# First layers of q and k as seven block products, v centered in its weights, and a plan ranked by kinds of steps

## The chip, the cores and the metric

The kernel runs on one core of a Trainium2 chip. The metric is the device time of that core in microseconds, the median of several runs. The engines are called PE (TensorE, the matrix engine), DVE (VectorE), ACT (ScalarE), POOL (GpSimd) and SP (SyncE, which here only issues transfers). PEld is PE's loading of weights, which overlaps its matmuls. All data is float32.

## The reference

The input x has 4 sequences of 2048 tokens with 256 values each. Two layers follow each other, each added to its input and normalized.

```python
def _mlp(x, W1, b1, W2, b2):
    h = gelu(x @ W1 + b1)                     # exact gelu
    return h @ W2 + b2
q, k, v = _mlp(x, W1q, ...), _mlp(x, W1k, ...), _mlp(x, W1v, ...)
scores = (q @ k.T) / sqrt(256 * 512) * tril(ones)      # causal, without softmax
out = scores @ v
out = (out - mean(out)) * rsqrt(var(out) + 1e-5) * ln_w + ln_b
x = layernorm(x + out)

xn = layernorm(x) * ln_gamma + ln_beta         # soft mixture of 16 experts, 16 slots each
logits = unit(xn) * scale @ unit(mu)           # 256 logits a token
dispatch = softmax(logits over the 2048 tokens of a sequence)
combine  = softmax(logits over the 256 slots)
slot_in  = dispatch.T @ xn
slot_out = gelu(slot_in @ w1[e] + b1[e]) @ w2[e] + b2[e]
x = layernorm(x + combine @ slot_out)
```

The sequence is the unit over which tokens are dispatched: a slot sums over all tokens of one sequence.

## The kernel before

The 8192 tokens are worked in 16 groups of 512 (`W`), four to a sequence; a group is four chunks of 128 tokens (`G = 4`, `P = 128`). Everything is written once as steps, and a planner in the kernel's Python code (`Plan`) decides in which order the steps of each engine are emitted; on the chip each engine works through its own list strictly in that order and waits on semaphores.

**The planner.** `plan.step(engine, length, emit, reads, writes, ...)` records a step with an assumed duration. `plan.begin(base)` sets the rank from which the following steps count up by 0.01; a step that reads a PSUM bank gets 1.5 less. `run` repeatedly takes, for each engine, the ready step with the smallest key: its possible starting time plus `PATIENCE[engine]` times its rank, then the rank. `LATE` is the assumed delay until another engine sees a step's end, `TABLE` the price of switching ScalarE's function table. `plan.tag` gives a kind of buffer its places, and a step that needs a buffer waits until one is free. PSUM has eight banks: three `mm`, two `tp`, three `at`.

**A group, in `attend`.** `load_x` brings the group's rows (`row`) and, by eight block transfers, the same tokens in a form that DVE's 32x32 transpose (L795) turns into `xT`, 128 input values by 512 tokens in two halves. L810 multiplies `xT` by W1q, W1k and W1v: for each of them two output halves `m`, each a sum over two input halves `k`, with 512 tokens as the moving side:

```python
for k in range(KC):
    nc.tensor.matmul(ph.place, wa[f"W1{n}"][:, k, m * P : (m + 1) * P], xT[:, k, :],
                     start=(k == 0), stop=(k == KC - 1))
```

L820 reads the bank with bias and gelu on ACT into `hid`. The second layers of q and k are folded into one matrix (`fold`, `wqk_sb` in `both_sb`), so that L833 makes `kt` from hidden k, and q is hidden q itself. L843 adds on DVE. `turn_group` sends `kt` through a bounce in DRAM (SP) and DVE's transpose (L542) back as `kT`. L860 and L871 make `vt`. L885 gives the scores of a chunk with itself, masked by L896. Everything before the chunk comes from running states: L912 multiplies `kt` and `vt`, L928 adds to `state`; L945 and L954 sum the bias's part of a chunk, which goes through DRAM and back into `a` and `run` (L960 to L969), where POOL adds (L979). L995 and L999 make the output of a chunk, L1010 adds it to `a`, L561 and L562 (`means`) take its mean and variance on DVE, and L1022 centers it and multiplies by `lnw`.

**The rest of a group.** `norms`: POOL adds `ln_b` to the row (L1041), takes roots by a power (L550), DVE joins (L1064), the next norm follows (L561 again, or, for the last two groups, squares on ACT at L571), centering on ACT and DVE (L664, L669), then gamma and beta on POOL (L1127, L1139) and squares on ACT (L1155). `back`: the logits (L1201), DVE's scaling (L1211), the smallest (L1223), and ACT's exponentials for combine (L1234), which go through DRAM. After each fourth group `softmaxes` (L1312, L1324), `slots` (L1346 sums the slots' inputs, then the experts) and `finish` (L1572 combines, L1580 adds, the last norm, the store).

**What sets the order around the change.** PE's list mixes groups: while one group's first layers run, the earlier group's scores, states and logits are interleaved. SP's list holds all transfers in one order. At the start, `load_x(0)`, the weights (W1q and W1v, W2q from ACT's queue, W1k, W2k, W2v from SP's), `load_x(1)`, `fold` (L746, L754, L768, L778), `unit_mu` (L704, L712, L691, L730) and `load_experts` come, each with its rank.

Of the kernel before, what the change touches and what calls it, by code (L numbers as in the profile page):

```python
# [8 lines left out]
F32 = mybir.dt.float32  # L9
# [5 lines left out]
P = 128  # L15
G = 4
# [9 lines left out]
LAST = 2  # L26
PART = 2
# [29 lines left out]
class Plan:  # L57
# [4 lines left out]
    PATIENCE = {"PE": 0.0, "DVE": 0.0, "ACT": 0.0, "POOL": 0.0, "SP": 0.5, "IN": 0.0}  # L62

    def __init__(self):
        self.steps, self.places, self.order, self.free = [], {}, {}, set()
        self.base = self.count = 0.0

    def begin(self, base):

        self.base, self.count = base, 0.0  # L70

# [13 lines left out]
    def step(self, engine, length, emit, reads=(), writes=(), table=None, holds=(), port=False):  # L85
# [3 lines left out]
        s = Step(engine, length, emit, self.base + self.count, table)  # L89
        s.holds = list(holds)  # L90
# [4 lines left out]
        if any((a[0] if isinstance(a, tuple) else a).tag.startswith("ps_") for a in reads):  # L95
            s.rank -= 1.5
        for accesses, write in ((reads, False), (writes, True)):
# [24 lines left out]
    def run(self):  # L122
# [26 lines left out]
        while left:  # L149
# [38 lines left out]
            free[e] = end  # L188
# [39 lines left out]
def kernel(  # L228
# [43 lines left out]
    for tag, n, shape in (  # L272
        ("row", 8, [G, C + 1]),
        ("xT", 2, [KC, W]),
        ("hid", 5, [KC, W]),
# [10 lines left out]
        ("lg", 7, [G, ES]),  # L286
        ("mx", 1, [ES]),
        ("ct", 5, [EH, W]),
# [20 lines left out]
    bank_places("mm", 3)  # L309
    bank_places("tp", 2)  # L310
    at_banks = bank_places("at", 3)
# [4 lines left out]
    def load_x(t):  # L316
# [15 lines left out]
        plan.step("SP", {0: 2.5, 1: 6.0, 2: 4.0}.get(t, 0.5), emit, writes=[xt])  # L332
# [5 lines left out]
        xs = plan.buffer("xT", KC)  # L338
# [14 lines left out]
        plan.step("SP", 4.8, emit_blocks, writes=[xs])  # L353
# [14 lines left out]
    )  # L368
    mu_sb = const.tile([P, KC, ES], F32, name="mu_sb")
# [29 lines left out]
    def load_experts():  # L399
# [20 lines left out]
        for n, length, emit in (  # L420
            ("w1", 7.0, emit_w1), ("w2", 2.2, emit_w2), ("b2", 10.1, emit_b2)
        ):
            plan.tag(n, [w1_sb])
            arrivals[n] = plan.buffer(n)
            plan.step("SP", length, emit, [], [arrivals[n]])
# [3 lines left out]
    for n, after in (  # L429
# [5 lines left out]
        plan.step("IN", after, lambda: None, [], [arrivals[n]])  # L435
    plan.tag("wqk", [mu_sb])
    arrivals["wqk"] = plan.buffer("wqk")
# [49 lines left out]
    def flips(src, at=None, dst=None):  # L487

        for h in range(2):
            pt = plan.buffer("ps_tp")  # L490
# [8 lines left out]
            plan.step("PE", G * _FLIP, flip, [src], [pt], holds=[dst] if dst else ())  # L499
            yield h, pt  # L500

    def transpose_group(src, dst, engines, at=None):
        for h, pt in flips(src, at, dst):
# [3 lines left out]
            plan.step(engines[h], length, emit, [pt], [(dst, [h])])  # L507
# [12 lines left out]
    def turn_out(src, of=None):  # L520
# [7 lines left out]
        plan.step("SP", 0.65 * (2 if of else 1), emit, [src], [bounce])  # L528
        return bounce

    def turn_in(bounce, dst):
# [8 lines left out]
        plan.step("SP", 2.2, emit, [bounce], [dst])  # L540
        plan.step(
# [4 lines left out]
    def inv_root(v, n):  # L546
# [7 lines left out]
        plan.step("POOL", 1.04 if n == G else 0.75, emit, [v], [r])  # L554
        return r

    def means(src, st, mv, c, access):
# [6 lines left out]
        plan.step("DVE", 0.6, emit, [src], [(st, [c]), (mv, [c])])  # L564

    def squares_of(src, mv, c, access):
# [9 lines left out]
        plan.step("ACT", 0.6, emit, [src, (mv, [c])], [(mv, [G + c])])  # L576

    def root_of(mv, cs, factor, add):
# [12 lines left out]
        plan.step("POOL", 0.25, emit, [(mv, cs)], [negm])  # L591
# [12 lines left out]
        plan.step(  # L604
# [5 lines left out]
    def center_by(dst, r, nm, engines, c0=0):  # L610

        for i, engine in enumerate(engines):
# [14 lines left out]
            plan.step(  # L627
# [6 lines left out]
    def center(dst, mv, r):  # L634

        for c in range(G):
# [7 lines left out]
            plan.step("DVE", 0.42, emit, [mv, r], [(dst, [c])])  # L644

    def center_on(dst, mv, r, engines, c0=0):
# [4 lines left out]
        plan.step(  # L651
# [7 lines left out]
        for i, engine in enumerate(engines):  # L659
# [14 lines left out]
            plan.step(  # L674
# [4 lines left out]
    def spread(col):  # L679
# [7 lines left out]
        plan.step("DVE", 0.56, emit, [col], [dg])  # L687
# [8 lines left out]
        plan.step("PE", _pe(ES), emit, [dg], [row])  # L696
        return row

    def unit_mu():
# [6 lines left out]
        plan.step("POOL", 1.1, emit, [muw], [mu2], port=True)  # L706
# [10 lines left out]
        plan.step("PE", 0.9, emit, [mu2], [pss])  # L717
# [6 lines left out]
        plan.step("DVE", 0.17, emit, [pss], [ms])  # L724
# [9 lines left out]
        plan.step("DVE", 0.96, emit, [row], [muw])  # L734

    def fold():
# [3 lines left out]
        for i, n in enumerate(("W2q", "W2k")):  # L740
            pt = plan.buffer("ps_tp")
# [9 lines left out]
            plan.step("PE", 4 * _FLIP, emit, [arrivals[n]], [pt])  # L751
# [10 lines left out]
            plan.step("DVE", 0.7 + 0.1 * (not i), emit, [pt], [f])  # L762
        for m in range(KC + 1):
# [11 lines left out]
            plan.step("PE", 2 * _pe(C + 1), emit, [f], [pw])  # L775
# [6 lines left out]
            plan.step("DVE", _dve(C), emit, [pw], [arrivals["wqk"]])  # L782

    a_tiles, n_tiles, l_tiles, c_tiles, t_tiles = {}, {}, {}, {}, {}
    state, run = [None], [None]

    def attend(t):
# [3 lines left out]
        if t in xs_tiles:  # L791

            xT = xs_tiles.pop(t)
            plan.step(
# [3 lines left out]
        else:  # L798
            xT = plan.buffer("xT", KC)
            transpose_group(xt, xT, ("DVE", "ACT"))  # L800

        hid = {}
        for i, n in enumerate("qkv"):
            hid[n] = plan.buffer("hid", KC)
            for m in range(KC):
                ph = plan.buffer("ps_mm")

                def emit(n=n, m=m, ph=ph):
# [6 lines left out]
                plan.step(  # L815
                    "PE", KC * _pe(W), emit, [xT, arrivals[f"W1{n}"]], [ph], holds=[hid[n]]
                )

                def emit(i=i, n=n, m=m, ph=ph):
                    nc.scalar.activation(  # L820
                        hid[n][:, m, :], ph.place, AF.Gelu,
                        bias=cols_sb[:, 4 * i + m : 4 * i + m + 1],
                    )

                plan.step("ACT", _act(W, 1), emit, [ph], [(hid[n], [m])], table="gelu")
        qT = hid["q"]
        kt = plan.buffer("kt", G)
        for c in range(G):
            pk = plan.buffer("ps_mm")

            def emit(c=c, pk=pk):
                for k in range(KC):
                    nc.tensor.matmul(  # L833
                        pk[:, : C + 1], hid["k"][:, k, c * P : (c + 1) * P], wqk_sb[:, k, :],
# [3 lines left out]
            plan.step(  # L838
                "PE", 2 * _pe(C + 1), emit, [hid["k"], arrivals["wqk"]], [pk], holds=[kt]
            )  # L840
            plan.step(
# [12 lines left out]
        for c0 in range(0, G, 2):  # L854
            pv = plan.buffer("ps_mm")

            def emit(c0=c0, pv=pv):
                for j in range(2):
                    for k in range(KC):
                        nc.tensor.matmul(  # L860
                            pv[:, j * C : (j + 1) * C],
                            hid["v"][:, k, (c0 + j) * P : (c0 + j + 1) * P],
# [3 lines left out]
            plan.step(  # L866
# [810 lines left out]
```

## Time and profile before

| what | value |
|---|---|
| median of 3 runs | 657.66 us (657.54 to 657.99) |
| span of the profiled execution, its own time | 656.7 us |
| busy PE, PEld, DVE, ACT, POOL | 644.6, 482.2, 482.8, 265.7, 308.6 us |
| L810, each of W1q, W1k, W1v | 128 instructions, 60.0, 58.2, 59.8 us |
| L820 ACT, 128x512, 96 times | 685 ns each |
| L1155 ACT, 128x256, and reading its accumulator, 64 times | 414 and 188 ns |
| L485 ACT copy of 128x512 | 589 ns |
| L928 DVE addition of 128x512, 56 times | 677 ns |
| L561, L562 DVE statistics on `a`, 64 times | 423 and 182 ns |
| L979 POOL addition of 128x256 | 741 ns |
| transfers | 85.24 MB, mean 130 GB/s |

The span runs from the first instruction to the last; the profiled execution has no other time of its own than this span, and the median of the runs is 1.0 us above it. A float32 matmul appears as two instructions. The mean duration that a group of matmuls shows includes the overlap of one with the next, so the price of one is read from a run of them in the chain of work that ended last.

### The profile page before, as it was taken

To read this page: it belongs to the slowest core of one execution; us is meant where nothing else is said; L and a number is where in the kernel's file an instruction comes from. 1 tells how busy PE (TensorE), PEld (TensorE's weight loads), DVE (VectorE), ACT (ScalarE), POOL (GpSimd) and SP (SyncE) were. 2 spreads that over 40 slices of the span, in tenths; PEclk is the share of its full clock that TensorE was granted. 3 is DMA by queue.
4 is the path that set the end of the run, shared out by engine and by line. 5 is a ranking of instruction groups with operands and counts; after the bars stand their busy time and mean duration, and the time that the engine had idled before them with its cause. 6 is when DMAs were issued, how large, how long until landed. Compare 5 with 4: busy or idle time off the path is not lost.

```text
span 656.7 us, 9472 instructions
## 1 busy us (share of the span) xinstructions
PE 644.6 (98%) x2964; PEld 482.2 (73%) x2964; DVE 482.8 (74%) x1295; ACT 265.7 (40%) x610; POOL 308.6 (47%) x407
## 2 busy tenths in 40 slices
PE   8999999999999999999999999999999999999995
PEld 6667767676768876857776877777776877887874
DVE  1448696868782987788796498688979689875686
ACT  3121343325255227051627212624244634536575
POOL 4415825251529145643517503757252927547234
PEclk9999999999999999999999999999999999999998
DMA  8967567765864267966677352794969672310374
GB/s 247 207 147 205 112 149 118 145 113 123 140 145 78 54 107 224 195 124 126 128 146 137 72 117 52 225 204 96 152 136 156 109 153 50 78 35 1 78 148 160
DMA packets 326458, 85.24 MB, mean 130 GB/s; under 512 B 257292, under 2 KB 324168, under 8 KB 326408
## 3 DMA queue, kind: packets, MB, share of 16 engines
q1 hardware_dynamic: 325304, 83.58, 60.5%
q10 hardware_dynamic: 960, 0.80, 0.4%
q8 instruction: 23, 0.38, 0.3%
q0 software_dynamic: 144, 0.26, 0.1%
q14 instruction: 27, 0.22, 0.1%
HBM read 52.57 MB, written 32.04 MB: 129 GB/s over the span
## 4 chain that ended last, share of the span: by engine, by line
PE 92%; ACT 1%; DVE 1%; DMA 1%; issue 1%; SPq 1%; POOL 1%; POOLq 0%; DVEq 0%; ACTq 0%
PE mm L810 25%; PE mm L1201 8%; PE at L1346 8%; PE mm L833 8%; PE at L912 8%; PE mm L860 8%; PE at L995 7%; PE at L1572 6%; PE at L885 4%; PE at L999 4%; PE at L945 1%; ACT squares L571 1%; DMA row<-in_x_dram 1%; DMA xnT<-bounce 1%; POOL root L601 1%
## 5 line engine op out<-in xcount | busy, mean ns | idle before, releaser
L820 ACT ACTIVATE hid<-mm,cols_sb 128x512 f32<-128x512 f32 x96 | 65.0, 685 | 194.2 <-PE mm L810 194.0
L550 POOL TENSOR_TENSOR root<-ve,nhalf 128x4 f32<-128x4 f32 (+1 forms) x39 | 41.2, 1058 | 143.8 <-DVE ve L1054 55.5
L995 PE MATMUL at<-state,hid 128*128 128x256 f32 x240 | 61.6, 379 | 0.0
L810 PE MATMUL mm<-xT,W1v_sb 128*128 128x512 f32 x128 | 59.8, 593 | 0.7 <-DVE both_sb L778 0.7
L912 PE MATMUL at<-vt,kt 128*128 128x256 f32 x240 | 60.4, 384 | 0.0
L810 PE MATMUL mm<-xT,W1q_sb 128*128 128x512 f32 x128 | 60.0, 596 | 0.2 <-DVE xT L484 0.2
L833 PE MATMUL mm<-both_sb,hid 128*128 128x257 f32 x256 | 59.2, 380 | 0.0
L1346 PE MATMUL at<-row,lg 128*128 128x257 f32 x256 | 58.2, 381 | 0.4 <-ACT lg L1324 0.4
L860 PE MATMUL mm<-W2v_sb,hid 128*128 128x256 f32 x256 | 58.5, 379 | 0.0
L1201 PE MATMUL mm<-mu_sb,xnT 128*128 128x256 f32 x256 | 58.1, 380 | 0.3 <-DVE xnT L542 0.3
L810 PE MATMUL mm<-xT,W1k_sb 128*128 128x512 f32 x128 | 58.2, 592 | 0.0
L1572 PE MATMUL at<-so,ct 128*128 128x256 f32 x256 | 57.6, 380 | 0.1
L1234 ACT ACTIVATE xn<-lg,nrm 128x256 f32<-128x256 f32 x64 | 31.9, 499 | 61.8 <-DVE lg L1211 61.8
L1201 PEld LDWEIGHTS mm<-mu_sb,xnT 128*128 128x128 f32 x256 | 48.4, 190 | 10.3 <-issue 2.6
L1572 PEld LDWEIGHTS at<-so,ct 128*128 128x128 f32 x256 | 48.2, 190 | 9.7 <-DVE st L561 1.2
L833 PEld LDWEIGHTS mm<-both_sb,hid 128*128 128x128 f32 x256 | 48.3, 190 | 8.9 <-issue 1.6
L995 PEld LDWEIGHTS at<-state,hid 128*128 128x128 f32 x240 | 45.4, 190 | 12.1 <-issue 6.5
L1346 PEld LDWEIGHTS at<-row,lg 128*128 128x128 f32 x256 | 47.9, 190 | 8.4 <-ACT lg L1324 1.0
L912 PEld LDWEIGHTS at<-vt,kt 128*128 128x128 f32 x240 | 44.6, 190 | 12.2 <-issue 5.4
L860 PEld LDWEIGHTS mm<-W2v_sb,hid 128*128 128x128 f32 x256 | 48.3, 190 | 7.1 <-DVE vt L871 0.4
L1041 POOL TENSOR_TENSOR row<-row,rows_sb 128x512 f32<-128x512 f32 x32 | 38.1, 1210 | 16.8 <-DMA row<-in_x_dram 11.7
L1251 POOL TENSOR_TENSOR sum<-sum,ss 128x4 f32<-128x4 f32 x16 | 4.0, 252 | 85.9 <-DVE ss L1247 70.9
(150 smaller groups left out, 1220.5 us busy)
## 6 DMA issues: line engine op xcount, KB each, us to landing
bounce<-xn SPq DMA_DIRECT2D x30, 512.0 KB
row<-in_x_dram SPq DMA_DIRECT2D x16, 512.0 KB
ct<-bounce SPq DMA_DIRECT2D x64, 128.0 KB
xT<-in_x_dram SPq DMA_DIRECT2D x120, 64.0 KB
bounce<-kt SPq DMA_DIRECT2D x30, 256.0 KB
kT<-bounce SPq DMA_DIRECT2D x60, 128.0 KB
out_dram<-row SPq DMA_DIRECT2D x15, 512.0 KB
xnT<-bounce SPq DMA_DIRECT2D x56, 128.0 KB
```

Of the source, the lines that this page charges most:

```text
L550: nc.gpsimd.tensor_tensor(r[:, :n], v[:, :n], nhalf.to_broadcast([P, n]), ALU.pow)
L810: nc.tensor.matmul(ph.place, wa[f"W1{n}"][:, k, m * P : (m + 1) * P], xT[:, k, :], start=(k == 0), stop=(k == KC - 1),)
L820: nc.scalar.activation(hid[n][:, m, :], ph.place, AF.Gelu, bias=cols_sb[:, 4 * i + m : 4 * i + m + 1],)
L833: nc.tensor.matmul(pk[:, : C + 1], hid["k"][:, k, c * P : (c + 1) * P], wqk_sb[:, k, :], start=(k == 0), stop=(k == KC - 1),)
L860: nc.tensor.matmul(pv[:, j * C : (j + 1) * C], hid["v"][:, k, (c0 + j) * P : (c0 + j + 1) * P], wa["W2v"][:, k, :], start=(k == 0), stop=( ...
L912: nc.tensor.matmul(pds[:, m * C : (m + 1) * C], kt[:, c, m * P : (m + 1) * P], vt[:, c, :], start=True, stop=True,)
L995: nc.tensor.matmul(po[:, :C], qT[:, k, toks[c]], s[:, k, :], start=(k == 0), stop=False,)
L1041: nc.gpsimd.tensor_tensor(row[:, c : c + PART, :C], row[:, c : c + PART, :C], lnb_r[:, :PART], ALU.add,)
L1201: nc.tensor.matmul(pl[:, j * ES : (j + 1) * ES], xnT[:, k, (c0 + j) * P : (c0 + j + 1) * P], mu_sb[:, k, :], start=(k == 0), stop=(k == KC ...
L1234: nc.scalar.activation(by_halves(cb)[:, :, c, :], lg[:, c, :].rearrange("p (h e) -> p h e", h=EH), AF.Exp, bias=nrm[:, c : c + 1], scale=-1.0,
L1346: nc.tensor.matmul(psi[:, : C + 1], lg[:, c, h * P : (h + 1) * P], row[:, c, :], start=(i == 0), stop=(i == n - 1),)
L1572: nc.tensor.matmul(pc[:, :C], ct[:, h, c * P : (c + 1) * P], so_t[:, h, :], start=(h == 0), stop=(h == EH - 1),)
```

## The change

**Seven products.** From group 1 on (`FIRST = 1`) q's and k's first layers are made block by block. The weights of one projection are four blocks (two input halves `k` by two output halves `m`), the tokens of a group four blocks (two input halves by two halves `lo` and `hi` of 256 tokens). Instead of eight products of blocks, seven are made, of sums and differences of blocks, by the same trick for q and k at once, so that one bank holds 256 columns of q and 256 of k. `mix_weights` makes three mixed weight blocks per projection once (DVE), `mix_last` replaces one block of W1q and W1k after group 0. `mix_tokens` makes four differences of token blocks per group on POOL (one in place). `project_mixed` has the products: the bank `sums` gets products 1, 3, 5 and 6, one on top of the other, and between them ScalarE copies what is in it (`keep`), and at last reads it (`activate2`); the banks `one` (product 2) and `two` (4, 7) are added by DVE to the copies (`add`); the gelu then works on those in place. `hid` for q and k becomes `hqk`, with two places for both; v keeps L810's form and has two places.

**Centering v.** `center_v` subtracts from each row of W2v, and from b2v, its own mean, once. The mean of the attention's output over the 256 values is then zero: `means` on `a` and the subtraction of the mean go away. The variance is the sum of squares, made on ACT (`attend12`, with an accumulator) and divided by 256 in `norms3`; `attend13` only multiplies by `lnw`.

**The plan.** Each step has a name; `plan.begin` gives a phase too. A table `SHIFTS` adds a number to the rank of each kind of step. `PATIENCE` is now 0.035 for ACT (0 before) and 0 for SP (0.5 before). `OVERLAP` lets the next step of an engine begin a little before the end of the one before. The banks are four `mm`, one `tp`, three `at`; the second of two transposes uses an `at` bank. `lg` has 6 places for 7, `ct` 4 for 5. In the emitted order of SP all rows' loads and the experts' weights now come ahead of the first bounce of `kt`, and `b2`'s 16 loads ahead of the first return of the running sums.

```diff
+SHIFTS = {
+    "": {"load_experts1": -80.298},
+    "attend": {"activate1qk": 1.52, "activate2qk": 5.949, "activate3qk": -0.301,
...
+}
+FIRST = 1
+STR_V = False
+ACC = False
+TENG = 'POOL'
+MM, TP, AT = 4, 1, 3
...
-    PATIENCE = {"PE": 0.0, "DVE": 0.0, "ACT": 0.0, "POOL": 0.0, "SP": 0.5, "IN": 0.0}
+    OVERLAP = {"PE": 0.0, "DVE": 0.075, "ACT": 0.09, "POOL": 0.06, "SP": 0.0, "IN": 0.0}
+
+    PATIENCE = {"PE": 0.0, "DVE": 0.0, "ACT": 0.035, "POOL": 0.0, "SP": 0.0, "IN": 0.0}
...
+        s.rank += SHIFT.get(s.kind, 0.0)
...
-            free[e] = end
+            free[e] = max(at, end - self.OVERLAP[e])
...
-        ("hid", 5, [KC, W]),
+        ("hqk", 2, [2, KC, W]),
+        ("hid", 2, [KC, W]),
+        ("xs", 1, [3, W // 2]),
...
-        ("lg", 7, [G, ES]),
+        ("lg", 6, [G, ES]),
...
-        ("ct", 5, [EH, W]),
+        ("ct", 4, [EH, W]),
...
+    def mix_weights():
+        def emit(w, s):
+            for to, a, b, op in (
+                (s[:, 0, :], w[:, 0, P:], w[:, 1, P:], ALU.add),
+                (s[:, 1, :], s[:, 0, :], w[:, 0, :P], ALU.subtract),
+                (s[:, 2, :], w[:, 1, :P], s[:, 1, :], ALU.subtract),
+            ):
+                nc.vector.tensor_tensor(to, a, b, op)
...
+    def mix_tokens(xT):
...
+        less(1, y(0), x(0, hi), x(0, lo), [(xT, [0, 1])], [(xs, [0])])
+        less(2, y(1), x(1, hi), y(0), [(xT, [3]), (xs, [0])], [(xs, [1])])
+        less(3, x(0, hi), x(1, hi), x(0, hi), [(xT, [3])], [(xT, [1])])
+        less(4, y(2), x(1, lo), y(1), [(xT, [2]), (xs, [1])], [(xs, [2])])
...
+        def product(name, bank, weights, tokens, reads, new):
+            def emit():
+                for j, i in enumerate(ids):
+                    nc.tensor.matmul(
+                        bank[:, j * N : (j + 1) * N], weights(i), tokens(),
+                        start=(new and not j), stop=True, skip_group_check=True,
+                    )
...
+        product(f"1{part}", sums, own(0, 0), x(0, lo), given + [(xT, [0])], True)
+        product(f"2{part}", one, own(1, 0), x(1, lo), given + [(xT, [2])], True)
+        keep(f"1{part}", sums, 0, 0, lo)
+        add(f"1{part}", one, 0, 0, lo)
+        product(f"3{part}", sums, mixed(1), y(1), [wm, (xs, [1])], False)
+        keep(f"2{part}", sums, 0, 1, hi)
+        product(f"4{part}", two, mixed(0), y(0), [wm, (xs, [0])], True)
+        product(f"5{part}", sums, own(0, 1), x(0, hi), given + [(xT, [1])], False)
+        keep(f"3{part}", sums, 1, 1, hi)
+        add(f"2{part}", two, 1, 1, hi)
+        for i in ids:
+            activate(f"1{part}", i, 1, None, hi, [])
+        product(f"6{part}", sums, own(1, 1), y(2), given + [(xs, [2])], False)
+        product(f"7{part}", two, mixed(2), x(1, hi), [wm, (xT, [3])], False)
+        for j, i in enumerate(ids):
+            activate(f"2{part}", i, 1, lambda j=j: sums[:, j * N : (j + 1) * N], lo, [sums])
+        add(f"3{part}", two, 0, 1, hi)
+        for i in ids:
+            activate(f"3{part}", i, 0, None, slice(0, W), [])
...
+    def center_v():
+        w, b = wa["W2v"], rows_sb[:, 0, :]
...
-            means((a, [c]), st, mv, c, lambda c=c: a[:, c, :])
...
-                nc.vector.scalar_tensor_tensor(
-                    a[:, c, :], a[:, c, :], mv[:, c, 0:1], lnw_r[:, 0, :],
-                    ALU.subtract, ALU.mult,
-                )
...
+                nc.scalar.activation(
+                    squares.rearrange("p k d -> p (k d)"), a[:, c, :], AF.Square,
+                    accum_out=mv[:, c, 1:2],
+                )
+
+            plan.step("attend12", "ACT", 0.6, emit, [(a, [c])], [(mv, [c])])
...
+                nc.vector.tensor_tensor(a[:, c, :], a[:, c, :], lnw_r[:, 0, :], ALU.mult)
```

In the changed kernel's own lines, the products are L953, `keep` L969, `add` L976, the subtractions of `mix_tokens` L924, the gelu L1067, v's first layer L1080, `kt` L1111, the scores L1163, the squares of `a` L1308.

## The prediction

> **What bounds the kernel now.** I read the page first (busy shares, clock, chain), then the windows, then the chain in order of time for the price of one matmul, then the groups for the other durations.
>
> ```profile
> PE 644.6 (98%) x2964; PEld 482.2 (73%) x2964; DVE 482.8 (74%) x1295; ACT 265.7 (40%) x610; POOL 308.6 (47%) x407
> ...
> PEclk9999999999999999999999999999999999999998
> ...
> PE 92%; ACT 1%; DVE 1%; DMA 1%; issue 1%; SPq 1%; POOL 1%; POOLq 0%; DVEq 0%; ACTq 0%
> ```
>
> TensorE is busy for 98% of the span at the full clock, and 92% of the chain that ended last is TensorE. Nothing else is near: VectorE has 174 us idle, ScalarE 391 us.
>
> ```profile
> 400.00:500.00 100.00, 100.00 (x436) 73.60 (x435) 80.72 (x217) 39.60 (x88) 51.69 (x64) 1.00 0.73 152
> ...
> 640.00:657.00 17.00, 8.77 (x41) 7.38 (x39) 10.33 (x36) 9.88 (x31) 7.36 (x20) 0.86 0.44 155
> ```
>
> The columns are PE, weight loads, DVE, ACT, POOL. In the middle PE has no idle time; only the start and the last 8 us are not PE's. So a shorter PE sum shortens the kernel one for one, as long as nothing makes PE wait.
>
> ```profile
> 182.53 3.45 PE mm L1201 x16
> ...
> 188.47 3.43 PE mm L810 x8
> ```
>
> These are lines of the chain in order of time. Eight 512-column instructions take 3.43 us (0.429 each), sixteen 256-column ones 3.45 us (0.216 each): PE's time goes by columns, and half the width costs half. A float32 matmul is two instructions here: L810 has 64 W1q matmuls in the code and 128 in the page.
>
> **The sum of the PE work removed.** Before, q and k of one group are 2 x 4 matmuls of 512 columns: 16 instructions x 0.429 = 6.86 us. After, 2 x 7 of 256 columns: 28 x 0.216 = 6.05 us. That is 0.82 us a group; groups 1 to 15 have it: **-12.2 us**. The changed kernel's order on PE confirms the count: 72 matmuls of 512 columns for 192, 904 of 256 for 694, all other shapes equal. The 28 weight loads are 0.190 us each under matmuls of 0.216; the L1201 row is exactly such a stream (a new weight for every 256 columns), so no price is added there.
>
> **What goes to the other engines, per group.**
> ScalarE: three `keep` copies of 128x512 from PSUM, 0.589 each by the L485 copies: 1.77. Four 256-wide and two 512-wide activations stand for four 512-wide ones; a 256-wide one lies between the squares' 0.414 (L1155) and the exponentials' 0.499 (L1234), I take 0.457, the middle: 4 x 0.457 + 2 x 0.685 - 4 x 0.685 = +0.46. The squares of the attention output: 4 x (0.414 + 0.188 for reading the accumulator) = 2.41. Together 15 x 2.23 + 16 x 2.41 = 72 us: 266 becomes 338 us, 52%.
> VectorE: three adds of 128x512 at 0.677 (L928) are +2.03; four statistics pairs at 0.423 + 0.182 (L561, L562) are -2.42; four products with lnw at 0.473 (L1223) for 0.514 (L1022) are -0.16. With some 6 us of one-time mixing and centering the engine stays at about 480 us.
> GpSimd: four `less` subtractions, 0.741 each by L979: 15 x 2.96 = 44 us, so 353 us.
> None of the three comes near the 632 us that PE keeps. All this work is hidden by PE as long as the round trips below are; without that cover each group pays for its longest wait.
>
> ```profile
> 55.45 2.50 POOL L1041 TENSOR_TENSOR row<-row,rows_sb 128x512 f32<-128x512 f32 x2 [0.24 <-DMA row<-in_x_dram]
> 55.46 1.55 DVE L1064 SCALAR_TENSOR_TENSOR row<-a,root,row 128x256 f32<-128x256 f32 x1
> ```
>
> This timeline shows a DVE instruction of mean 0.517 us take 1.55 beside a POOL instruction that began 0.01 us before. If every new POOL instruction held DVE up for its whole 0.741 us, DVE would get 60 x 0.741 = 44 us more: 525 us, still 107 us under PE. I take a quarter of it, since most L1064 rows are not lengthened (the mean is 0.517), and price it at nothing for PE. The Trainium skill, SBUF — State Buffer, section SBUF: two separate sides, states that a DVE instruction with two SBUF inputs and a GpSimd instruction exclude each other on a shared port pair, the loser waiting for the whole instruction; it speaks against putting the subtractions on GpSimd, and by it the full 44 us would be the reading.
>
> **The new round trips.** The bank `sums` is used four times in a row: product 1, `keep1` on ScalarE, product 3, `keep2`, product 5, `keep3`, product 6, `activate2`. PE waits at 3, 5 and 6 until ScalarE has copied. What a trip needs is 0.3 us from PE's end to ACT's start (the copy of L820 began 0.3 us after the fourth L810 ended in the first projection), 0.59 for the copy and about 0.1 back: 1.0 us. What the changed order queues on PE in between, priced by the rows above: 1.73 us between 1 and 3 in every group; between 3 and 5 from 1.1 (groups 7, 11) and 1.3 (15) over 1.7 to more; between 5 and 6 1.73 in five groups and 3 to 6 in the others. `add2` and product 7 have 3.5 us and more, the k activations before the next L1111 3.5 us and more. Behind a waiting product on PE stands everything, so a late trip is a loss for the whole kernel; queued ahead of a `keep` on ACT is mostly the 0.37 us `cs` copy, in four groups (3, 6, 10, 14) a table load (1.28) and an exponential. Thirty-one trips have a cover under 1.8 us. The bounds: 0 (all covered) and, if each met the table load, exponential and read-out of 1.97 us, 31 x (1.0 + 1.97 - 1.73) = 38 us. The order has such a head in four, so I lie near the low end: 4 x 0.3 = **+1.2 us**.
>
> **The start.** In DVE's new order six 128x128 operations stand ahead of the copy of xT (L484, 6.95 us); the second three wait for W1k, whose last packet the trace has at 6.76 us. At 0.28 each (L685) the copy begins at 7.65: +0.7. Then the unit norm's matmuls, moved up behind the first half of W1q, wait for GpSimd's square of mu, which ended at 10.57 before: PE is there at 10.1, +0.5. The 0.7 us that L810 waited for DVE's both_sb (L778) is covered now by W1k's and W1v's halves that stand in between: -0.7. Sum **+0.5 us**.
> On SP's queue all remaining row loads (six of 512 KB for two), w1 and w2 now stand ahead of the first bounce of kt: 2.1 MB more. At the page's 207 to 247 GB/s of the first slices that is 9 us; against it the block load of group 2 went behind the bounce, the PE work between kt and the scores grew from 16.1 to 17.4 us, and kT was 1.8 us early (L542 ended at 40.94, L885 began at 42.76). Bounds: 0 and 9 - 1.8 - 1.3 = 6. I take **+1.0**, near the low end, because the DMA row of the first 40 us falls to 5 and 3 tenths from 26 to 28 us. The 16 loads of b2 now also precede the return of the running sums by 7.8 us, on which L979, then DVE, then the `at` banks wait; PE has some 14 us of other work from the first score matmul to the next need of that.
>
> **The end.** The last 16 combines, their sums and stores are the same instructions; the fillers in front of the last expert step sum to 9.4 us of PE for 9.35. Price 0, bounds -1 and +1.
>
> Sum, against the profiled execution's own 656.7 us: -12.2 + 1.2 + 0.5 + 1.0 = -9.5, so 647.2; the median of the runs is 1.0 us over that span, so **648.2 us**.
>
> **The rivals.**
> (a) Early transfers: the 6 us bound instead of 1: 653.2. For it: the DMA engines were at 9 tenths from 17 to 26 us. Against it: the larger cover. 8%.
> (b) Trips late by a little everywhere: 31 x 0.2 = 6.2 instead of 1.2: 653.2. For it: ScalarE goes from 40 to 52% with the same strict order. 6%.
> (c) Slower than before, one mechanism: ScalarE's order. The squares of `a` (`attend12`) stand ahead of `keep1`, and they wait for DVE's `a`, which waits for GpSimd's sums and the returned DMA (POOL L979 waited up to 12.9 us for it). Where that is late, `keep1` and so PE wait. PE has 8.4 us of work from the last output matmul of a group to product 3, and the way through DVE (L1010, 0.42) and ACT (two squares of 0.60 and the `cs` copy) needs about 2. It decides from 0.65 us a group (9.5 / 15) of additional wait; at 1.2 us a group it is 648.2 + 18 = 666 us. Against it: DVE keeps its 26% of idle time. 5%.
> (d) The block products cost PE as much as before, since each half-width matmul has its own cost: 28 x 0.245 would be needed instead of 0.216; L1201, L860 and L833 speak against it. Then 648.2 + 12.2 = 660. 2%.
>
> **How the numbers follow.** The forecast has 78%, 645 to 652. Range: below, all trips covered, the start at nothing and the end at -1: 657.7 - 12.2 - 1 = 644.5; above, (a) or (b) whole: 653.2 and the end's +1, 654. Within 0.2% of the time before (656.3 to 659.0, about what a measurement of this kernel can tell from no change) lies only the gap between (b) and (d). Faster 0.92 (the forecast, (a), (b)), slower 0.07 (c and d), same 0.01.
>
> **What would show it.** Right: PE busy near 632 us, still 98% of a span of 647; L810 with 72 matmuls and the products (L953) at 0.216 a step; ACT near 338, POOL near 353 us. Each step: the W1q matmul at 8.4 us, no wait of some us of PE for DMA before 45 us, PE's waits for `keep` (L969) under 2 us in all. Wrong if PE's sum falls by 12 and its idle time rises by as much: then the waits name ACT (L969), POOL (L924) or a transfer.

## The result, and the profile after

The changed kernel took **665.42 us** (median of 4 runs, 664.99 to 665.97) against 657.60 us of the kernel before on the same chip: ratio 1.0112, interval 1.0099 to 1.0126. The forecast was 648.2 us. The profiled execution has a span of 663.3 us, 6.6 more than before.

The page of the changed kernel: engine sums, granted TensorE clock in 40 slices, shares of the chain that ended last, and the group of the `keep` copies.

```profile
PE 638.3 (96%) x3144; PEld 518.1 (78%) x3144; DVE 478.8 (72%) x1227; ACT 326.0 (49%) x813; POOL 349.5 (53%) x467
...
PEclk9999999999899999999999999999999999998997
...
PE 77%; DVE 8%; DMA 5%; SPq 4%; POOL 2%; issue 1%; ACT 1%; POOLq 0%; DVEq 0%; ACTq 0%
...
L969 ACT COPY hqk<-mm 128x512 f32<-128x512 f32 x45 | 26.4, 586 | 58.5 <-PE mm L953 58.1
```

TensorE's share of the chain fell from 92% to 77%: VectorE, DMA and the sync queue took it. Two 8s and a 7 stand in a clock row that was all 9 before the last slice. The `keep` copies waited 58.1 us for TensorE; no wait of TensorE for them is in the trace.

Windows of the changed kernel (columns: PE, weight loads, DVE, ACT, POOL, clock, DMA share, GB/s):

```profile
20.00:60.00 40.00, 37.21 (x159) 27.20 (x160) 17.39 (x34) 11.21 (x23) 22.74 (x31) 1.00 0.80 188
100.00:200.00 100.00, 96.85 (x446) 78.71 (x445) 75.18 (x184) 50.00 (x128) 47.06 (x62) 0.97 0.74 127
400.00:500.00 100.00, 99.17 (x494) 80.42 (x494) 77.61 (x200) 50.05 (x119) 50.02 (x66) 1.00 0.70 148
580.00:610.00 30.00, 27.34 (x151) 22.65 (x150) 15.55 (x47) 15.31 (x43) 18.63 (x24) 0.94 0.06 18
640.00:664.00 24.00, 12.71 (x58) 10.47 (x56) 13.73 (x49) 12.75 (x37) 7.75 (x21) 0.84 0.57 181
```

TensorE has holes in a few places, and two windows ahead of the tail have a clock under 1. The granted clock is 0.5 for 6.83 us from 165.0 us, where the largest hole is about to end, and for 3.41 us from 598.5 us, just behind three holes. The whole difference adds up (idle time counted from TensorE's first instruction on):

| from the two traces, us | before | after | difference |
|---|---|---|---|
| PE busy, less the time lost at clock 0.5 (after: half of 6.0 and of 3.4 busy us) | 644.6 | 633.6 | -11.0 |
| lost at clock 0.5 ahead of the last product | 0 | 4.7 | +4.7 |
| PE idle ahead of its last product (holes of 0.1 us and more) | 2.6 | 13.0 | +10.3 |
| behind the last product | 7.9 | 10.6 | +2.6 |

That is +6.6. The saving is there, and waits took it with interest. The products themselves, in the chain in order of time:

```profile
51.07 1.73 PE mm L953 x8
...
99.74 3.45 PE mm L953 x16
```

Both are 0.216 us each, as forecast. Now the largest hole, in the timeline of the changed kernel (start, us, engine, line; SPq is the issue of transfers on the sync queue; in brackets the idle time before and what ended it):

```profile
148.56 4.29 SPq L635 DMA_DIRECT2D ct<-bounce  x4
...
152.95 3.48 SPq L635 DMA_DIRECT2D kT<-bounce  x4
...
156.48 3.81 SPq L635 DMA_DIRECT2D xnT<-bounce  x4
...
163.81 1.25 DVE L642 STREAM_TRANSPOSE xnT<-xnT 128x1024 f32<-128x1024 f32 x1 [4.50 <-DMA xnT<-bounce]
...
165.09 0.68 DVE L976 TENSOR_TENSOR hqk<-mm,hqk 128x512 f32<-128x512 f32 x1
...
165.82 1.65 PE L1495 MATMUL mm<-mu_sb,xnT 128*128 128x256 f32 x3 [3.15 <-DVE hqk L976]
```

Three returns stand one behind the other on the sync queue, 0.9 to 1.1 us an issue, so xnT lands at 163.8. VectorE idles 4.50 us for it, with its transpose at the head of its queue, and behind that stands the add that frees TensorE's bank. The releaser named is that add (L976); the cause is two steps further back, the order on the sync queue (f2 below tests this). The start of the changed kernel:

```profile
19.98 4.37 SPq L418 DMA_DIRECT2D row<-in_x_dram  x5
...
27.14 4.19 SPq L626 DMA_DIRECT2D bounce<-kt  x2
...
31.43 7.31 SPq L441 DMA_DIRECT2D xT<-in_x_dram  x8
...
41.20 1.25 DVE L1047 STREAM_TRANSPOSE xT<-xT 128x1024 f32<-128x1024 f32 x1 [5.99 <-DMA kT<-bounce]
...
42.55 1.96 PE L1080 MATMUL mm<-xT,W1v_sb 128*128 128x512 f32 x4 [1.28 <-issue]
...
46.01 1.16 PE L1163 MATMUL at<-hqk,kT 128*128 128x128 f32 x8 [1.51 <-DVE kT L642]
```

Five row loads go out at 20 us; the two stores of kt behind them need 4.19 us to issue, and the blocks of group 2 and kT come late: 2.8 us of holes. (Eight of the sixteen row loads stand ahead of the first bounce of kt, against four before; not all of them, as the section on the change has it: the other eight go out from 273 us on.) Two smaller holes are at 296 and 451 us. This is the second:

```profile
446.52 2.50 POOL L1332 TENSOR_TENSOR row<-row,rows_sb 128x512 f32<-128x512 f32 x2 [2.10 <-DMA row<-in_x_dram]
446.58 2.72 DVE L1358 SCALAR_TENSOR_TENSOR row<-a,root,row 128x256 f32<-128x256 f32 x2
...
451.95 1.12 PE L1080 MATMUL mm<-xT,W1v_sb 128*128 128x512 f32 x2 [0.83 <-DVE hqk L976]
```

A row came late on GpSimd, and its addition there began beside two VectorE instructions whose median is 0.477 us each: they took 2.72 us together, VectorE had no pause from there to the add (L976), and TensorE waited for that. At 296 us the same lines stand (2.77 us, hole 0.88). The end, one line of the kernel before and then the changed kernel:

```profile
585.27 10.17 PE L1346 MATMUL at<-row,lg 128*128 128x257 f32 x46
```

```profile
595.54 6.59 POOL L1606 TENSOR_TENSOR lg<-lg,dg 128x512 f32<-128x512 f32 x5 [0.56 <-ACT dg L1595]
...
595.94 1.37 DVE L1409 TENSOR_TENSOR xn<-xn,rows_sb 128x256 f32<-128x256 f32 x1
...
597.23 0.98 DVE L1701 TENSOR_SCALAR siT<-tp,gb_sb 128x256 f32<-128x256 f32 x2
...
597.82 1.82 PE L1716 MATMUL mm<-w_sb,siT 128*32 128x128 f32 x32 [1.54 <-DVE siT L1701]
```

In the changed kernel TensorE has run out of slot sums here (the last ones ahead end at 593 us), waits 0.48, 0.62 and 1.54 us in the chain of the last batch's softmax and slots, and then runs at half clock.

### The profile page after: what moved, and what is told of

The parts are those of the page before. It is cut to its first block, busy times and chain, and to the rows that moved or that the text cites. A ratio compares the mean times of both kernels' runs of the same rounds, so it can differ in the third digit from the quotient of the medians.

```text
span 663.3 us, 10176 instructions
## 1 busy us (share of the span) xinstructions
PE 638.3 (96%) x3144; PEld 518.1 (78%) x3144; DVE 478.8 (72%) x1227; ACT 326.0 (49%) x813; POOL 349.5 (53%) x467
## 4 chain that ended last, share of the span: by engine, by line
PE 77%; DVE 8%; DMA 5%; SPq 4%; POOL 2%; issue 1%; ACT 1%; POOLq 0%; DVEq 0%; ACTq 0%
PE mm L953 12%; PE at L1640 9%; PE mm L1495 8%; PE mm L1080 7%; PE mm L1111 7%; PE mm L1138 7%; PE at L1282 7%; PE at L1193 6%; PE at L1163 4%; PE at L1286 4%; SPq L635 3%; PE at L1866 3%; DVE row L1874 2%; DVE st L661 2%; DMA bounce<-xn 2%; DMA row<-in_x_dram 1%
## 5 line engine op out<-in xcount | busy, mean ns | idle before, releaser
L1495 PE MATMUL mm<-mu_sb,xnT 128*128 128x256 f32 x256 | 62.4, 394 | 3.2 <-DVE hqk L976 3.2
L1080 PE MATMUL mm<-xT,W1v_sb 128*128 128x512 f32 x128 | 60.6, 596 | 3.0 <-DVE hqk L976 1.7
L1282 PE MATMUL at<-state,hqk 128*128 128x256 f32 x240 | 61.6, 379 | 0.0
L1495 PEld LDWEIGHTS mm<-mu_sb,xnT 128*128 128x128 f32 x256 | 50.4, 198 | 11.6 <-DVE hqk L976 3.6
L1111 PE MATMUL mm<-both_sb,hqk 128*128 128x257 f32 x256 | 58.8, 379 | 0.0
L1308 ACT ACTIVATE squares<-a 128x256 f32<-128x256 f32 x64 | 26.5, 414 | 63.4 <-DVE a L1297 45.2
L969 ACT COPY hqk<-mm 128x512 f32<-128x512 f32 x45 | 26.4, 586 | 58.5 <-PE mm L953 58.1
L1111 PEld LDWEIGHTS mm<-both_sb,hqk 128*128 128x128 f32 x256 | 48.6, 190 | 7.4 <-issue 0.5
L1282 PEld LDWEIGHTS at<-state,hqk 128*128 128x128 f32 x240 | 45.3, 190 | 10.4 <-issue 4.5
L764 ACT ACTIVATE row<-row,root,root 128x256 f32<-128x256 f32 x60 | 31.9, 591 | 34.8 <-DVE root L753 33.2
L1209 DVE TENSOR_TENSOR state<-at,state 128x512 f32<-128x512 f32 x56 | 37.9, 677 | 10.7 <-PE at L1193 10.2
```

The lines of the kernel that those rows point to most:

```text
L1111: nc.tensor.matmul(pk[:, : C + 1], hqk[:, 1, k, c * P : (c + 1) * P], wqk_sb[:, k, :], start=(k == 0), stop=(k == KC - 1),)
L1209: nc.vector.tensor_add(new_v, pds.place, old.place.rearrange("p k d -> p (k d)"))
L1282: nc.tensor.matmul(po[:, :C], hqk[:, 0, k, toks[c]], s[:, k, :], start=(k == 0), stop=False,)
L1495: nc.tensor.matmul(pl[:, j * ES : (j + 1) * ES], xnT[:, k, (c0 + j) * P : (c0 + j + 1) * P], mu_sb[:, k, :], start=(k == 0), stop=(k == KC ...
```

## The experiments

Theory: the saving is real, and the order of a few instructions (transfers on the sync queue above all) opens holes, each of which can cost the clock too. Rivals: the round trips of the products (B), or centred v with its buffers (C). Every ratio is to the kernel before on the same chip, with its interval. "Idle" below is TensorE's idle time in holes of 0.1 us and more, from its first instruction to its last product. The files of f2 and later have some lines more: L652 there is L635 here, L1512 is L1495, L1180 is L1163.

**Parts of the change undone.** The first two without the ranks by kind:

```
-SHIFT = {f"{phase} {kind}": by for ...}
+SHIFT = {}
 # e2 also: OVERLAP all 0.0; PATIENCE ACT 0.0, SP 0.5
```

> The changed kernel with no ranks by kind (the table of shifts empty); seven products, centred v, buffers and the new planner constants stay. Theory A (the order that the ranks set leaves TensorE waiting in a few places, and the saving of 12 us is real): the holes at 41, 162 and 593 us go, 648 to 655 us, TensorE's idle time before the last product under 6 us. Rival B (the round trips of the seven products cost it, whatever the order): 662 to 668 us. Rival C (centred v, squares on ScalarE, the smaller buffers cost it): 662 to 668 us too, B and C then told apart by the kernels with eight products. Rival D (the ranks hold the new products together): over 668 us.

> As the last, and the planner's constants of before as well (no overlap of 0.06 to 0.09 us, no pull of the rank on ScalarE, 0.5 on the sync queue). Theory A: 647 to 655 us, within 3 us of the kernel without ranks. If the sync queue's own constant (rank no longer counted, so that loads go out as soon as they can) made the late transfers: this one at least 4 us below the kernel without ranks. Rivals B and C: 662 to 668 us.

Then eight products in all groups, with the ranks and without:

```
-FIRST = 1
+FIRST = 99      # and no mix_weights, no mix_last
 # e4 also: SHIFT = {}
```

> The changed kernel with eight block products everywhere (the first layers of q and k as in group 0; no mixed weights, no differences on GpSimd, no adds on VectorE), ranks, centred v and buffers kept. Theory A: the holes stay or move, and 12 us of products come back: 668 to 678 us. Rival B: the waits that the seven products brought go, 656 to 661 us. Rival C: 664 to 672 us.

> Eight products, no ranks: of the change only centred v with its squares on ScalarE, the buffers, the banks and the planner's constants are left. Theory A: 656 to 661 us, like the kernel before. Rival B: the same, 656 to 661 us. Rival C: 664 us or more.

| | ranks | time, us | ratio to before | idle, us |
|---|---|---|---|---|
| seven (the change) | yes | 665.42 | 1.0112 | 13.0 |
| seven | no | 687.98 | 1.0458 [1.0400, 1.0517] | 30.3 |
| seven, old constants | no | 682.78 | 1.0368 [1.0335, 1.0401] | 26.4 |
| eight | yes | 689.86 | 1.0475 [1.0445, 1.0505] | 23.9 |
| eight | no | 667.56 | 1.0145 [1.0110, 1.0180] | 8.9 |

Theory A failed in all four (648 to 655, 647 to 655, 668 to 678 and 656 to 661 us were expected): without the ranks there are more holes, not fewer, as rival D had said, and e4 came where rival C had put it (664 us or more). And seven products without ranks are 20 us slower than eight without ranks, while doing 12 us less on TensorE. The ranks fit only the program that they were made with: with eight products they leave one hole of 10.9 us at 623 us. In e1 the largest hole is again a return: kT, issued at 169.5 us behind ct, the sums and a store on the sync queue (5.29 us). And in e2 TensorE did wait for the `keep` copies (total us, times, longest):

```profile
PE mm L953 <- ACT hqk L969: 5.4, 8, 0.8
```

So the round trips of rival B are not free of themselves; in the changed kernel, where no such wait is in the trace, the order hides them. The theory had to be tested hole by hole.

**The hole and the clock.** f1 fills the hole at 162 us with products that change nothing; f2 moves one transfer.

```
 # f1, in project(), v's first half of group 6
-for k in range(KC):
+for o, k in enumerate((0, 0, 1, 0, 1) if again else range(KC)):
 # f2, earliest planned time of one step
+NOT_BEFORE = {("finish turn_in1", 2): 152.0}
```

> The changed kernel; in group 6 the first half of v's first layer (the products just ahead of the 3.15 us hole at 162 us) is computed two and a half times, the same result each time: about 2.6 us of extra products where TensorE stood still. Theory K (an idle TensorE of 3 us also costs the half clock that follows it: 6.8 us at 0.5): the hole shrinks to about 0.6 us, the stretch at clock 0.5 between 165 and 172 us is gone, and the kernel is 3 to 4 us faster, 662 us, though it computes more. Rival L (the clock in the rows is only a record, the matmuls behind the hole take as long anyway): 665 us or up to 2.6 us more.

> The changed kernel; one transfer moved: the second return of the softmax weights (ct from the bounce, four DMAs, ahead of kT and xnT on the sync queue at 148.6 us) is planned no earlier than 152 us, behind both; TensorE's order is the same. Theory T (three returns in one row on the sync queue, 0.95 us an issue, bring xnT late; VectorE, whose transpose of xnT is at the head of its queue, holds the add that frees TensorE's bank): hole at 162 us under 0.5 us, no half clock there, 665 - 3.1 - 3.4 = 658 to 660 us. Rival (the bank or the add itself is late, whatever the transfers): the hole stays above 2 us, 664 to 667 us.

f1: 662.73 us, 2.7 less than the change though it computes 2.6 us more (ratio to before 1.0067, 1.0055 to 1.0078). The same windows, first of the changed kernel, then of f1 (columns: PE, clock, DMA share, GB/s):

```profile
155.00:175.00 20.00, 16.85 (x74) 0.83 0.71 83
```

```profile
155.00:175.00 20.00, 19.50 (x87) 1.00 0.68 93
```

More instructions pass in the same 20 us: the half clock is a cost and not only a record. K stands, L falls. f2: **658.14 us**, 7.3 less (1.0005, 0.9997 to 1.0014). Its timeline:

```profile
149.88 2.54 SPq L652 DMA_DIRECT2D kT<-bounce  x4
152.52 3.30 SPq L652 DMA_DIRECT2D xnT<-bounce  x4
155.87 3.85 SPq L652 DMA_DIRECT2D ct<-bounce  x4
...
161.92 3.62 PE L1512 MATMUL mm<-mu_sb,xnT 128*128 128x256 f32 x16
```

TensorE goes straight into the products with mu, and the half clock there is gone (this execution has it in two other places, 3.41 us each). Four DMAs in another place on one queue were worth 7 us.

**The early rows**, alone and together with f2:

```
+AFTER = {("load load_x1", t + 1): ("load load_x2", t), ...}   # t = 3..7
 # and norms1, norms2 of t behind the differences of group t
```

> The changed kernel; on the sync queue the rows of groups 3 to 7 (five loads of 512 KB, issued at 20 to 24 us) go out each behind the blocks of its own group instead, and GpSimd's additions on these rows behind that group's differences; TensorE's, VectorE's and ScalarE's orders are the same. Theory T (the early loads fill the DMA engines until 42 us, so that group 2's blocks and the first kT come late): the holes at 41 and 44.5 us (2.8 us together) go, 661.5 to 663.5 us. Rival (group 2's blocks wait for their buffer, not for the queue): both holes stay, 664 to 667 us.

> Both moves, the return of ct at 148.6 us behind kT and xnT and the rows of groups 3 to 7 later. Theory T: the sum of the two, 655 to 658 us, TensorE's idle time before its last product down from 14.4 us to about 8.5 us. If the holes only move to the next late transfer: 662 us or more.

f3: 662.35 us (1.0068, 1.0048 to 1.0088), as expected: 3.1 less, and in its timeline TensorE no longer waits here:

```profile
25.99 1.03 SPq L643 DMA_DIRECT2D bounce<-kt  x2
27.12 4.46 SPq L458 DMA_DIRECT2D xT<-in_x_dram  x8
31.63 2.81 SPq L652 DMA_DIRECT2D kT<-bounce  x4
```

```profile
41.11 1.88 PE L1097 MATMUL mm<-xT,W1v_sb 128*128 128x512 f32 x4
42.83 1.95 PE L1180 MATMUL at<-hqk,kT 128*128 128x128 f32 x16
```

Both together: 656.60 us (0.9981, 0.9971 to 0.9990), idle 6.7 us (8.1 with the 1.4 us ahead of TensorE's first instruction, which the expectation's 8.5 takes in), already a little below the kernel before. Closing these holes opened none of their size.

**Start, end, tail.** g1 moves three steps on single engines; g2 takes two ranks out of the last finish; g3 has everything.

```
 # g1
+("mix mix_weightsq", 1): ("attend attend2", 1), ("mix mix_weightsk", 1): ...
+("late slots slot_sums1", 28..31): ("part softmaxes1", 1)
+("end norms norms8", 4): ("late slots slots3", 2)
 # g2
-"end finish": {"center_by1": 598.422, ... "squares_of1": -146.947, ...
```

> On top of the kernel with both moves (656.6 us), three small moves in the order of single engines: VectorE mixes the weights of group 1 behind its copy of group 0's xT instead of ahead; four slot sums follow the transposes for the maxima of the last batch on TensorE instead of going ahead; VectorE adds the last rows of xn behind the copies of siT. Theory T (holes by order): TensorE starts 0.6 us earlier, the holes before the last batch's weights (0.5, 0.6 and 1.5 us at 585 to 589 us) shrink to 1 us together, so the clock cannot fall there: 653 to 655 us. Rival (these holes are the length of the softmax chain, not its order): 656 to 658 us.

> The kernel with both moves (656.6 us), and in the last batch's finish no ranks for the squares and for the centring on ScalarE, so that rows are centred and stored as they come. Theory T (the centring held back on ScalarE lets 2.6 MB of output out in one stretch, 643 to 651 us at 340 GB/s, behind the last product): the tail behind TensorE's last product falls from 10.5 us to about 8 us, 653.5 to 655 us. Rival (the tail is the chain add, squares, root, centring of the last rows, whatever the stores): 656 to 657 us.

> All moves together: the return of ct, the rows, the start, the softmax of the last batch, the tail. Theory T: 650 to 652.5 us, faster than the kernel before by about 6 us; TensorE's idle time ahead of its last product about 5 us, no half clock before the tail. Rival (a change of the order in one place opens holes in others): over 655 us.

g1: 655.52 us (0.9959, 0.9942 to 0.9977). The wait for siT fell from 1.54 to 0.64 us and the one for xT at the start from 1.51 to 0.35 us, but 1.08 us of waiting for the unit norm came up at 9.3 us. g2: 655.74 us (0.9968, 0.9956 to 0.9979), the time behind the last product 9.1 us instead of 10.5. Both gained about 1 us and ended between the range of the theory and that of the rival; the interval of g2 overlaps that of f4, so its gain rests on the tail in the trace. g3: **654.65 us** (0.9944, 0.9931 to 0.9958), the fastest here and faster than both kernels, idle 4.5 us; it missed its 650 to 652.5. The span of its profiled execution is 650.5 us, its runs took 652.2 to 655.1 (the last section says what I think of this spread). Where the tail goes shows in the DMA view from 635 to 664 us (40 slices), first of the changed kernel, then of g3, whose last product ends at 641.4 us:

```profile
DMA  8995999999999920000000000059999999999000
```

```profile
DMA  0004960595000899999400000000000000000000
```

In the changed kernel the whole output of the last finish goes out in one piece behind the last product; in g3 part of it leaves earlier.

**Are the products on the path?** The order of f4, with the fourth block product done twice.

```
+def twice():
+    emit()
+    if name[0] == "4":
+        emit()
```

> The kernel with both moves (656.6 us) and its order, with an eighth product put back in groups 1 to 15: the fourth block product of q and k is computed twice, the same result (30 more pairs... 60 matmuls of 256 columns, 0.216 us each: 13 us). Theory T (the saving of the seven products lies on the path of TensorE once the holes are closed): 12 to 13 us more, 668 to 670 us. Rival (the kernel is bound by its order and transfers, so that a product more or less moves it little): under 663 us.

669.18 us (1.0179, 1.0161 to 1.0197): 12.6 us more than f4. The page of g4 against 634.0 us of PE in f4:

```profile
PE 648.6 (97%) x3204; PEld 527.2 (79%) x3204; DVE 481.6 (72%) x1227; ACT 325.9 (49%) x813; POOL 350.9 (53%) x467
```

So the forecast's largest term is right: with the large holes closed, the eighth product costs its TensorE time one for one (60 instructions of 0.216 us are 13.0). Rival B falls for this order: the saving arrives, and neither here nor in f4 does TensorE wait for `keep`; in the order of e2 it did.

**Which part made the holes?** Centred v alone on the kernel before; the old weight of ranks on the sync queue in the changed kernel; eight products without ranks with the old constants, and that with the old banks or one more buffer.

```
 # h1: before.py with center_v(), AF.Square on ScalarE, one multiplication
 # h2: -PATIENCE "SP": 0.0   +"SP": 0.5
 # h3: FIRST = 99, SHIFT = {}, OVERLAP 0.0, PATIENCE as before
 # i1: h3 with MM, TP, AT = 3, 2, 3 and both transposes in ps_tp
 # i2: h3 with  -("lg", 6, [G, ES])   +("lg", 7, [G, ES])
```

> The kernel before, with centred v alone: the mean taken out of W2v and of its bias row at the start, the squares of the attention output on ScalarE, one multiplication on VectorE for the centring; eight products, buffers, banks and planner as before. Theory (this part is off the path of TensorE, which it neither gives nor takes anything): 656 to 659 us. Rival C (squares on ScalarE stand ahead of its activations and hold TensorE's banks): over 661 us.

> The changed kernel with the weight of the rank on the sync queue back at 0.5, as before (one constant); everything else as changed, the ranks by kind too. Theory T (with weight 0 a load goes out as soon as its buffer is free, so five rows go ahead of the first returns): the holes at 41 and 44 us go, 658 to 664 us. Rival (the ranks by kind fit only the order that they were made with): over 667 us.

> Eight products, no ranks, and the planner's constants as before: of the change only centred v, the buffers and the banks are left. If the planner's constants made the 10 us that the eight products without ranks lost: 656 to 660 us. If the buffers and banks (four mm, one tp, six lg, four ct) or centred v made them: 664 us or more; the kernel before with centred v alone then tells which.

> Eight products, no ranks, the planner's constants as before, and the PSUM banks as before too: three for products, two for transposes, both halves of a transpose in these (the change: four, one, and the second half in a bank of the attention). If the banks made the 10 us that this kernel loses with the banks of the change (667.6 us): 657 to 661 us. If not: 665 us or more.

> Eight products, no ranks, the planner's constants as before, and seven buffers for the softmax weights lg as before instead of six (the mixed weights and differences, which eight products don't use, give the space). If the missing buffer made the 10 us: 657 to 662 us, and the 3.8 us hole ahead of the slot sums of the last batch (598 us) goes. If not: 665 us or more.

h1: 659.23 us (1.0017, 1.0008 to 1.0026): VectorE 37 us less, ScalarE 35 us more, TensorE 644.6 us as before, and about 1 us more idle at the start. Centred v costs 1.3 us, clear of noise but small; rival C falls in that half. h2 missed: 679.02 us (1.0308, 1.0292 to 1.0323), where its rival had put it, with a new hole of 6.9 us ahead of the scores at 292 us and 1.79 us still at 41 us. The theory's reason was wrong too, since the rows still go out early:

```profile
18.13 6.58 SPq L418 DMA_DIRECT2D row<-in_x_dram  x6
```

With the ranks (also in e3) six row loads go out here, without them (e1, e2, e4, h3) one: it is the table of ranks, with -822 for `load_x1`, that sends the rows early, and not the constant. (e2 lies 5.2 us under e1, as its expectation had it for this constant, but other constants went back with it; h2, which sets this one alone, went the other way.) h3: 667.65 us (1.0148, 1.0132 to 1.0163), so the planner's constants are innocent of the 10 us. i1: 670.59 us (1.0180, 1.0154 to 1.0206), so are the banks. i2: 661.08 us (1.0033, 1.0017 to 1.0050): one buffer for the softmax weights gives 6.6 of the 10 us back (7.6 by the ratios). The wait that it shortens, first in h3, then in i2:

```profile
602.62 3.79 PE L1640 MATMUL at<-row,lg 128*128 128x257 f32 x8 [3.81 <-ACT lg L1618]
```

```profile
599.39 4.02 PE L1640 MATMUL at<-row,lg 128*128 128x257 f32 x11 [1.71 <-ACT lg L1618]
```

So the other half of rival C, the buffers, stands for eight products: the change took that buffer while it added hqk, the differences and the mixed weights. The changed kernel itself was not tried with seven lg, and the fewer places of `ct` and `hid` were not tried at all.

## Why the prediction was wrong, step by step

- **The PE work (-12.2)** was right within 1.2 us: -11.0 between the traces, and 12.6 us with the eighth product back.
- **The round trips (+1.2, bounds 0 to 38)**: 0. TensorE never waited for `keep`, so the prediction's rivals (b) and (c) did not happen. That (c) stands at 666 us, near the 665.4 measured, is luck. In e2, the same products in another order, the trips cost 5.4 us.
- **The start (+0.5)**: +1.0. The first W1q matmul came at 8.30 us (8.4 forecast).
- **The early transfers (+1.0, bounds 0 to 6)**: 2.8 us of holes, 3.1 us by f3. The mechanism was seen, and taken too near the low end: the bound's cover was counted on kT alone, while the blocks of group 2 came late as well.
- **The end ("price 0, bounds -1 and +1")** failed. It was priced by its instructions, which are the same; their order is not. Before, slot sums (L1346) filled TensorE without a break until 595 us and again between the transposes behind; in the new order they are spent by 593 us, so the softmax chain lies open (2.6 us against 0.4), and the tail is 2.6 us longer because the output leaves late (g2, which changes that order alone, takes 1.5 of it back; the rest stays open).
- **"All this work is hidden by PE"** is the step that failed most. It compared engine sums. It never walked the sync queue in the middle of the kernel, where three returns in a row at 162 us cost 3.15 us (f2 takes the hole away by moving one of them).
- **The shared port, priced "at nothing for PE"**, failed in a small way. The size was about right: VectorE's sum came to 478.8 us, not 525, and what its instructions took above the median of their line rose from 14.9 to 25.3 us between the traces, about the quarter of 44 us that was taken. But at 296 and 451 us such lengthened instructions, beside late rows on GpSimd, held TensorE 0.9 us each (before: one hole of 0.3). This is read from the trace; the two were not tried by themselves.
- **The clock** had no term at all: 4.7 us.

Forecast span 647.2; +1.2 work, -1.2 trips, +0.5 start, +1.8 early transfers, +3.2 at 162 us, +1.4 rows, +2.3 and +2.6 end and tail, -0.3 at the combines, +4.7 clock: 663.4, against 663.3 measured. The text's own line "Wrong if PE's sum falls by 12 and its idle time rises by as much" is nearly what happened (11.0 and 10.3); of the causes that it names, only the transfers came.

ScalarE was 12 us under the 338 forecast; VectorE (478.8) and GpSimd (349.5) were met. Another lengthened instruction is the L1409 above, 1.37 us beside GpSimd's L1606 where the one before took 0.42.

## What to carry to other kernels

When an engine that is 98% busy gets 2% less work and every list a new order, as here, the other queues lose their cover: walk the DMA-issuing queue and each strict queue in the new order, at the places where two transfers meet, instead of comparing engine sums. Look two steps behind the releaser that the trace names, for the transfer at the head of its engine's queue. After such a change, close the holes one by one, with a run for each, before judging the change: here six small moves turned +1.1% into -0.6%.

## What was not expected of the hardware

**The clock.** In the nineteen profiled executions every stretch of clock 0.5 ahead of the tail is a multiple of 3.413 us long, and within an execution all changes lie on one grid of that step. Sorting the windows of this grid that ran at full clock by TensorE's idle time in them: each of the 15 with more than 1.95 us idle was followed by a window at half clock, none with less than 1.45 us was, and of 25 between, 11 were (in the changed kernel 2.32 us idle in the window from 161.6 us and 2.12 in the one from 595.1 were enough). So about half a window of idle time, in one hole or several, costs at least half of the next window's work, 1.7 us. The Trainium skill, TensorE: Matmul & The Clock Gate, section Part 1: The HAM clock gate, gives the same window, says that it runs freely, and asks for at least one idle window; the length and the grid agree with these runs, the whole idle window does not. The three holes at the end of the changed kernel (2.6 us together) brought the half clock in its profile and not in those of f1 and f4, where they are as long. In f1 and f4 the grid splits them over two windows of 1.3 to 1.4 us idle each; in the changed kernel 2.12 us fall into one. I think that this also spreads the times of f4 and g3 over 3 to 4 us: the runs of g3 with a mean granted clock of 0.996 and 0.997 took 652.2 and 653.0 us, those with 0.992 and 0.993 took 654.4 to 655.1. It was not tried by itself.

**The sync queue.** An issue of a return took 0.6 us in f2 (kT) and 1.1 us for ct in the changed kernel, and the two stores of kt took 4.19 us to issue behind five row loads and 1.03 us without them (f3). So here a transfer put on the queue early was paid for by the issue behind it.
